# State space layer on one Trainium2 core: the product with C issued one group later, last states copied ahead of the exponentials, six scan buffers

## The chip, the cores and the metric

The kernel runs on one core of one Trainium2 chip. The core has four compute engines that each work through their own list of instructions in order and wait for each other by semaphores: PE (TensorE, matrix products and transposes), DVE (VectorE), ACT (ScalarE) and POOL (GpSimd). Transfers between the chip's main memory and the on-chip memory are issued from a fifth queue, SP. The metric is the device time of one execution in microseconds (us). Before the change it is 8284.29 us, the median of three runs that lay between 8283.61 and 8287.84 us.

## What is computed

The reference is a pair of layers on an image batch of 4 x 384 x 64 x 64 in float32. The second layer, windowed attention, isn't touched by the change. The first is a state space layer: each image is read as 4096 tokens of 384 channels, normalized, projected to 768 inner channels (xb) and 768 gates (z), convolved over four tokens, and passed through a recurrence with 16 states for every inner channel:

```python
xc  = silu(conv(xb) + conv_b)                 # (tokens, 768)
dt, Bm, Cm = split(xc @ x_proj_w.T)           # 24, 16 and 16 columns
dt  = softplus(dt @ dt_w.T + dt_b)            # (tokens, 768)
A   = -exp(A_log)                             # (768, 16)
def step(h, inp):                             # h: (768, 16), one token after another
    dt_t, B_t, C_t, x_t = inp
    dA  = exp(dt_t[:, :, None] * A[None])
    dBx = (dt_t * x_t)[:, :, None] * B_t[:, None, :]
    h   = dA * h + dBx
    y_t = einsum('bdn,bn->bd', h, C_t)
    return h, y_t
y   = (ys + xc * D) * silu(z)
out = y @ out_proj_w.T                        # back to 384 channels, added to the input
```

## The kernel before, as far as the change touches it

The kernel cuts every image into 16 chunks of 256 tokens, 64 chunks in all; the work of one chunk is called a step here. In a step the 768 inner channels are 6 blocks of 128 (one channel for each of the 128 partitions) and the 16 states are 4 groups of 4, so a step has 24 groups, numbered m. A group's scan results lie in a tile `hs` of 128 x (4 states x 256 tokens). Each group takes two slots of the kernel's hand-made schedule, one for each half (two states), so a step has 48 slots. These are the pieces that work on a group:

```python
def dt_x(I, d, h):                 # GpSimd: dt * x of a block
    h["dtx"][d] = ...
    nc.gpsimd.tensor_tensor(h["dtx"][d], dt_block, xc_block, ALU.mult)
def dt_x_copied(d, h):             # ScalarE: a copy in PSUM for VectorE
    nc.scalar.copy(dtx_ps[:, d % 2, :], h["dtx"][d])
def first_states(I, d, h):         # GpSimd: states at the chunk's first token, three small ops
    ...
def begun(I, m, h):                # ScalarE: those into column 0 of db
    nc.scalar.copy(dbs[I, m][:, :, 0], h["h0", d][:, g * NG : (g + 1) * NG])
def driven(I, m, h, eng):          # db = dt*x*B: 16 groups of a step on VectorE, 8 on GpSimd
    db = w2.tile([P, NG, T], F32, tag="db", ..., bufs=6)
    dtx = dtx_ps[:, d % 2, :] if eng is nc.vector else h["dtx"][d]
    eng.tensor_tensor(db[:, :, 1:], dtx..., h["B"][g][:, :, 1:], ALU.mult)
def decay(I, m, half, k, h):       # ScalarE: exp(dt * A) of one state into PSUM
    act(da_ps[half][:, k, 1:], h["dt"][...], AF.Exp, scale=nega[:, d, n : n + 1])
def scans(I, m, half, hs):         # VectorE: the recurrence of two states over 256 tokens
    nc.vector.tensor_tensor_scan(hs[:, pair, :]..., da_ps[half]..., dbs[I, m][:, pair, :]...,
                                 0.0, ALU.mult, ALU.add)
def kept_states(I, m, hs):         # ScalarE: the last token's states, for the next chunk
    nc.scalar.copy(state[:, d, g * NG : (g + 1) * NG], hs[:, :, T - 1])
def with_c(I, m, h, hs):           # GpSimd: hs *= C, in place
    nc.gpsimd.tensor_tensor(hs, hs, h["C"][m % (NS // NG)], ALU.mult)
def summed(I, m, h, hs):           # PE: sum over states, as 8 transposes that accumulate in PSUM
    for k in range(NG):
        for half in range(2):
            nc.tensor.matmul(y[:, d % 2, half, :], hs[:, k, ...], ident, is_transpose=True, ...)
```

Since `with_c` writes over `hs`, it may begin only when `kept_states` has copied the last column. `da_ps` has two tiles, one for each half. After two blocks are summed, `turn` takes the result back to channels: `out` (ScalarE copies the sums, tile `ys`), `back` (PE transposes them and adds xc * D), and `gated` (VectorE multiplies by silu(z), tile `yg`); in the next step the output projection reads `yg`. The loop that puts all of this in order is

```python
            for n in range(STEPS * M):
                I, m = divmod(n, M)
                hs = w2.tile([P, NG, T], F32, tag="hs", name=f"hs_{I}_{m}", bufs=5)
                for half in range(2):
                    others, acts = plan[I][2 * m + half]
                    if half == 0 and behind:
                        acts.insert(0, lambda last=behind[-1]: kept_states(*last[:2], last[3]))
                    if 2 * n + half + 1 < len(halves):
                        nxt = halves[2 * n + half + 1]
                        acts.insert(0, lambda nxt=nxt: decay(*nxt, 0, steps[nxt[0]]))
                        acts.insert(2, lambda nxt=nxt: decay(*nxt, 1, steps[nxt[0]]))
                    for what in acts:
                        what()
                    if half == 0:
                        if behind:
                            with_c(*behind[-1])
                        ready = len(behind) - 1
                        if ready == 1 and behind[0][1] % (2 * NS // NG) == 0:
                            ready = 0
                        for _ in range(ready):
                            summed(*behind.pop(0))
                    scans(I, m, half, hs)
                    for what in others:
                        what()
                behind.append((I, m, steps[I], hs))
```

`acts` is ScalarE's other work of a slot, `others` that of the other engines; both are filled from a table `AT` of slot numbers. So in the first slot of group n ScalarE does one exponential, the copy of group n-1's last states, the other exponential; GpSimd gets the product of group n-1, PE the sums of group n-2, VectorE the scan of group n.

Of the kernel before, what the change touches and what calls it, by code (L numbers as in the profile page):

```python
# [8 lines left out]
F32 = mybir.dt.float32  # L9
# [5 lines left out]
P = 128  # L15
# [7 lines left out]
NG = 4  # L23
# [3 lines left out]
T = 256  # L27
# [21 lines left out]
def two_layers(  # L49
# [45 lines left out]
    def act(o, i, func, **kw):  # L95
        ins = nc.scalar.activation(o, i, func, **kw)  # L96
        return in_order(ins) if func in tabled else ins
# [175 lines left out]
    def layer0(x1s, mvs, gms1):  # L273

        with ExitStack() as es:
# [7 lines left out]
            w2 = es.enter_context(tc.tile_pool(name="w2", bufs=2))  # L283
# [1 line left out]


            AT = {
             'norm': (11, 19, 19, 20, 20, 22, 26, 26, 30, 30, 32),
             'kept': -15,
             'x': ((-11, -11, -8, -7), (-11, -11, -7, -5), (-7, -6, -4, -3)),  # L290
             'c': ((-3, -2, 0, 5), (3, 3, 7, 8), (15, 16, 18, 19)),
             'z': ((1, 2, 3, 5), (10, 11, 14, 15), (8, 15, 16, 18)),
             'burst': (25, 28, 28, 31),
             'softplus': ((31, 33, 34, 36, 36, 37, 39, 39, 42),
                          (44, 47, 47, 50, 50, 51, 52, 52, 55),
                          (57, 60, 61, 61, 63, 65, 66, 66, 69)),
             'dtx': (-5, -3, 9, 13, 23, 29),
             'dtx_ps': (-3, 5, 10, 17, 24, 31),
             'driven': ((-4, 0), (-3, 1), (-1, 1), (-1, 1), (1, 0), (6, 0), (6, 1), (8, 1),
                        (10, 1), (11, 1), (14, 1), (15, 1), (18, 0), (19, 1), (23, 0), (25, 1),  # L300
                        (25, 0), (26, 1), (30, 0), (32, 1), (35, 1), (36, 0), (36, 1),
                        (41, 1)),
             'turn': (21, 24, 26),
             'out': (11, 17, 21, 23, 23, 24, 26, 27, 29, 30),
             'e0': (-4, -2, 11, 12, 23, 26),
             'h0': (-4, -1, 11, 16, 24, 32),
             'first': (-3, 0, 0, 4, 3, 7, 9, 10, 13, 14, 19, 18, 23, 23, 25, 27, 29, 30, 32, 33,
                       38, 41, 41, 46),
            }
            ACT = 1  # L310
# [48 lines left out]
            def bank(tag="mm", pool=ps):  # L359
                return pool.tile([P, 2, T], F32, tag=tag, name=f"{tag}_ps")  # L360
# [282 lines left out]
            def decay(I, m, half, k, h):  # L643

                d, g = divmod(m, NS // NG)
                n = g * NG + 2 * half + k
                act(
                    da_ps[half][:, k, 1:], h["dt"][d // 2][:, d % 2, 1:], AF.Exp,
                    scale=nega[:, d, n : n + 1],
                )  # L650

            def scans(I, m, half, hs):


                pair = slice(2 * half, 2 * half + 2)
                nc.vector.tensor_tensor_scan(  # L656
                    hs[:, pair, :].rearrange("p k t -> p (k t)"),
                    da_ps[half].rearrange("p k t -> p (k t)"),
                    dbs[I, m][:, pair, :].rearrange("p k t -> p (k t)"),
                    0.0, ALU.mult, ALU.add,  # L660
                )

            def kept_states(I, m, hs):
                d, g = divmod(m, NS // NG)
                nc.scalar.copy(state[:, d, g * NG : (g + 1) * NG], hs[:, :, T - 1])  # L665

            def with_c(I, m, h, hs):

                nc.gpsimd.tensor_tensor(hs, hs, h["C"][m % (NS // NG)], ALU.mult)  # L669

            def summed(I, m, h, hs):


                d, g = divmod(m, NS // NG)
                if d % 2 == 0 and g == 0:
                    h["yt"][d // 2] = ps_y.tile([P, 2, 2, P], F32, tag="y", name="y")
                y = h["yt"][d // 2]
                for k in range(NG):
                    first = g == 0 and k == 0
                    last = g == NS // NG - 1 and k == NG - 1  # L680
                    for half in range(2):
                        nc.tensor.matmul(  # L682
                            y[:, d % 2, half, :], hs[:, k, half * P : (half + 1) * P], ident,
                            is_transpose=True, start=(first and half == 0 and d % 2 == 0),
                            stop=(last and half == 1 and d % 2 == 1), skip_group_check=True,
                        )

            def turn(I, p, h, at, s):


                def out():
                    h["ys", p] = w2.tile([P, 2, 2, P], F32, tag="ys", name=f"ys_{I}_{p}")
                    nc.scalar.copy(h["ys", p], h["yt"][p])

                def back():
                    h["y", p] = bank()
                    for k in range(2):
                        y = h["y", p][:, k, :]
                        for half in range(2):
                            nc.tensor.matmul(  # L700
                                y[:, half * P : (half + 1) * P], h["ys", p][:, k, half, :], ident,
                                is_transpose=True, start=(k == 0 and half == 0), stop=False,
                                skip_group_check=True,
                            )
                        nc.tensor.matmul(
                            y, dsd[:, 2 * p + k, :], h["xc"][p][:, k, :], start=False,
                            stop=(k == 1), skip_group_check=True,
                        )

                def gated():  # L710
                    yg = w2.tile([P, 2, T], F32, tag="yg", name=f"yg_{I}_{p}", bufs=4)
                    nc.vector.tensor_tensor(yg, h["y", p], h["sz"][p], ALU.mult)
                    h["yg"].append(yg)

                for after, what, kind in zip(AT["turn"], (out, back, gated), (ACT, 0, 0)):
                    at(s + after, what, kind)
# [63 lines left out]
            for I in range(STEPS):  # L780
                h = steps[I]
# [43 lines left out]
            behind = []  # L825
            for n in range(STEPS * M):
                I, m = divmod(n, M)
                hs = w2.tile([P, NG, T], F32, tag="hs", name=f"hs_{I}_{m}", bufs=5)
                for half in range(2):

                    others, acts = plan[I][2 * m + half]
                    if half == 0 and behind:
                        acts.insert(0, lambda last=behind[-1]: kept_states(*last[:2], last[3]))
                    if 2 * n + half + 1 < len(halves):
                        nxt = halves[2 * n + half + 1]
                        acts.insert(0, lambda nxt=nxt: decay(*nxt, 0, steps[nxt[0]]))
                        acts.insert(2, lambda nxt=nxt: decay(*nxt, 1, steps[nxt[0]]))
                    for what in acts:
                        what()
                    if half == 0:  # L840
                        if behind:
                            with_c(*behind[-1])

                        ready = len(behind) - 1
                        if ready == 1 and behind[0][1] % (2 * NS // NG) == 0:
                            ready = 0
                        for _ in range(ready):
                            summed(*behind.pop(0))
                    scans(I, m, half, hs)
                    for what in others:  # L850
                        what()
                behind.append((I, m, steps[I], hs))
            with_c(*behind[-1])
            for what in behind:
                summed(*what)
            for slot in plan[STEPS]:
# [353 lines left out]
    mvs = [small.tile([P, NJ, 2], F32, tag="mv1", name=f"mv1_{b}", bufs=NB) for b in range(NB)]  # L1210
    gms = [small.tile([P, NJ, 2], F32, tag="gm1", name=f"gm_b{b}", bufs=NB) for b in range(NB)]
    layer0(x1s, mvs, gms)
    only0.close()
    layer1(x1s, mvs, gms)
# [46 lines left out]
```

## Time and profile before

| | before |
|---|---|
| time, median of 3 | 8284.29 us |
| span of the profiled execution | 8282.4 us |
| first layer | until about 5930 us of the span |
| PE busy | 7499.3 us, 91% of the span |
| GpSimd busy | 6954.3 us, 84% |
| VectorE busy | 6666.8 us, 80% |
| ScalarE busy | 6079.0 us, 73% |
| granted TensorE clock, mean | 0.963 |

The shares are averages over two layers with different limits, so the first layer has to be read from its own stretch of the trace. In a view of waits, "DVE hs L656 <- ACT da L96" says that the operation on VectorE which writes `hs` sat idle until ScalarE's operation on `da` ended; then come the total in us, the number of such waits, and the longest. In a timeline, each row is the start, the duration, the engine, the line of the kernel, the operation, what it writes and reads, and in brackets the engine's idle time just before it and what ended it. The lines that matter here are L669 (`with_c`), L665 (`kept_states`), L656 (`scans`), L637 (`driven`), L629 (`begun`), L622 to L625 (`first_states`), L603 and L609 (`dt_x` and its copy), L682 (`summed`), L705 and L712 (`back` and `gated`). L96 is a helper through which ScalarE's functions go, so those are told apart by their tiles.

### The profile page before, as it was taken

How to read it: one execution, taken by the hardware profiler on the slowest of the kernel's cores; microseconds unless marked ns; L12 is line 12 of the kernel's file. 1: busy time of each engine (PE TensorE's matmuls, PEld its weight loads, DVE VectorE, ACT ScalarE, POOL GpSimd, SP SyncE). 2: the span in 40 equal slices, each digit the busy share in tenths (PEclk: the TensorE clock that was granted, in tenths of full speed). 3: DMA queues.
4: the chain of work that ended last, by engine and by line, in shares of the span. 5: the costliest groups of instructions: out<-in, count | busy, mean ns of one | idle time of the engine just before them, and what ended most of it. 6: DMA issues, size and time to landing. Idle time of an engine off the chain costs nothing.

```text
span 8282.4 us, 144249 instructions
## 1 busy us (share of the span) xinstructions
PE 7499.3 (91%) x48570; PEld 5769.9 (70%) x48570; DVE 6666.8 (80%) x9783; ACT 6079.0 (73%) x17509; POOL 6954.3 (84%) x5223
## 2 busy tenths in 40 slices
PE   6898998899998989898989899899799999999999
PEld 5777777777777777777777777777555555555555
DVE  5888888888888888888888888888666666666666
ACT  4888888888888888888888888888555455455455
POOL 3999998989999898999989899999677777677777
PEclk9999999999999999999999999999799999999999
DMA  3212211221222122212211211121222233222322
GB/s 96 77 60 66 77 59 55 66 72 58 65 74 65 55 59 73 64 61 72 68 53 59 66 61 55 60 71 51 79 85 86 85 89 88 81 88 81 87 85 64
DMA packets 459624, 583.93 MB, mean 71 GB/s; under 512 B 195036, under 2 KB 343276, under 8 KB 458756
## 3 DMA queue, kind: packets, MB, share of 16 engines
q1 hardware_dynamic: 458884, 574.69, 22.7%
q8 instruction: 387, 6.34, 0.3%
q14 instruction: 353, 2.89, 0.1%
HBM read 472.02 MB, written 84.73 MB: 67 GB/s over the span
## 4 chain that ended last, share of the span: by engine, by line
PE 44%; ACT 21%; POOL 17%; DVE 12%; issue 5%; DMA 0%; SPq 0%; POOLq 0%; DVEq 0%; ACTq 0%
POOL hs L669 11%; ACT da L96 8%; DVE hs L656 6%; PE mm_ps L419 6%; PE y L682 5%; PE pt_ps L1047 4%; PE mm_ps L574 4%; PE mm_ps L426 3%; PE lg_ps L1016 3%; POOL db L637 3%; PE mm_ps L920 3%; PE mm_ps L1100 3%; PE mm_ps L953 3%; PE mm_ps L983 3%; PE pv_ps L1073 3%
## 5 line engine op out<-in xcount | busy, mean ns | idle before, releaser
L669 POOL TENSOR_TENSOR hs<-hs,C 128x1024 f32<-128x1024 f32 x1536 | 3622.9, 2363 | 478.4 <-ACT state L665 421.2
L656 DVE TENSOR_TENSOR_SCAN hs<-da,db 128x512 f32<-128x512 f32 x3072 | 3623.3, 1211 | 357.8 <-ACT da L96 210.2
L96 ACT ACTIVATE da<-dt,nega 128x255 f32<-128x255 f32 x6144 | 2898.3, 474 | 699.3 <-DVE hs L656 670.8
L1037 POOL TENSOR_SCALAR sg<-sg,rsum 128x308 f32<-128x308 f32 x1536 | 1621.4, 1076 | 638.9 <-DVE rsum L1035 637.2
L682 PE MATMUL y<-ident,hs 128*128 128x128 f32 x12288 | 1667.1, 283 | 468.1 <-POOL hs L669 450.5
L682 PEld LDWEIGHTS y<-ident,hs 128*128 128x128 f32 x12288 | 1443.1, 146 | 728.2 <-POOL hs L669 590.9
L637 DVE TENSOR_TENSOR db<-dtx_ps,B 128x1020 f32<-128x1020 f32 x1024 | 1223.1, 1200 | 110.9 <-ACT dtx_ps L609 105.7
L637 POOL TENSOR_TENSOR db<-dtx,B 128x1020 f32<-128x1020 f32 x512 | 1207.6, 2359 | 1.4 <-DMA B<-bcrows 1.4
L419 PE MATMUL mm_ps<-xn,w_in 128*128 128x256 f32 x4608 | 1160.5, 400 | 1.9 <-DVE xn L390 1.9
L96 ACT ACTIVATE sg<-sg,mx 128x308 f32<-128x308 f32 x1536 | 828.8, 541 | 250.8 <-DVE mx L1022 221.8
L419 PEld LDWEIGHTS mm_ps<-xn,w_in 128*128 128x128 f32 x4608 | 919.6, 206 | 132.3 <-DVE xn L390 2.6
L1022 DVE CUSTOM_DVE_ANT_0 sg<-lg_ps,bias 128x308 f32<-128x308 f32 x1536 | 643.2, 475 | 382.1 <-PE lg_ps L1016 382.1
L426 PE MATMUL mm_ps<-xb,dcv 128*128 128x256 f32 x3072 | 772.7, 400 | 9.4 <-DVE gm_b L270 9.4
L1065 ACT COPY tb<-pt_ps 88x512 f32<-88x512 f32 x384 | 222.3, 579 | 625.5 <-PE pt_ps L1061 625.4
L426 PEld LDWEIGHTS mm_ps<-xb,dcv 128*128 128x128 f32 x3072 | 592.0, 199 | 112.5 <-issue 19.9
L729 PE MATMUL mm_ps<-yg,w_out 128*128 128x256 f32 x2304 | 551.4, 380 | 0.0
L1052 DVE COPY ta<-pt_ps 110x512 f32<-110x512 f32 x768 | 492.7, 683 | 23.3 <-PE pt_ps L1047 23.3
L729 PEld LDWEIGHTS mm_ps<-yg,w_out 128*128 128x128 f32 x2304 | 434.3, 191 | 57.0
L1047 PE MATMUL pt_ps<-ident,sg 128*110 128x128 f32 x3072 | 417.6, 279 | 0.9 <-POOL sg L1037 0.8
L1047 PEld LDWEIGHTS pt_ps<-ident,sg 128*110 128x110 f32 x3072 | 322.8, 133 | 78.0 <-issue 48.4
L920 PE MATMUL mm_ps<-xn,w_qkv 128*128 128x512 f32 (+2 forms) x612 | 277.7, 592 | 60.4 <-DVE xn L907 53.2
L1016 PE MATMUL lg_ps<-k,q 32*128 32x308 f32 x3072 | 311.3, 473 | 0.0
(154 smaller groups left out, 10400.7 us busy)
## 6 DMA issues: line engine op xcount, KB each, us to landing
B<-bcrows SPq DMA_DIRECT2D x256, 512.0 KB
C<-bcrows SPq DMA_DIRECT2D x256, 512.0 KB
vw<-vd SPq DMA_DIRECT2D x1792, 33.0 KB
xr<-x SPq DMA_DIRECT2D x28, 1056.0 KB
vd<-v SPq DMA_DIRECT2D x280, 96.0 KB
xi<-in_x_dram SPq DMA_DIRECT2D x64, 384.0 KB
xo<-in_x_dram SPq DMA_DIRECT2D x64, 384.0 KB
x<-xo SPq DMA_DIRECT2D x64, 384.0 KB
```

What stands on the lines that cost most here:

```text
L96: ins = nc.scalar.activation(o, i, func, **kw)
L419: nc.tensor.matmul(pb[:, k, :], w_in[:, j, m * P : (m + 1) * P], xn[:, j, :], start=(j == 0), stop=(j == NJ - 1),)
L426: nc.tensor.matmul(pb[:, k, :], dcv[:, d, c, :], xb[:, d, c : c + T], start=(c == 0), stop=(c == KC - 1),)
L637: eng.tensor_tensor(db[:, :, 1:], dtx[:, 1:].unsqueeze(1).broadcast_to([P, NG, T - 1]), h["B"][g][:, :, 1:], ALU.mult,)
L656: nc.vector.tensor_tensor_scan(hs[:, pair, :].rearrange("p k t -> p (k t)"), da_ps[half].rearrange("p k t -> p (k t)"), dbs[I, m][:, pair, ...
L669: nc.gpsimd.tensor_tensor(hs, hs, h["C"][m % (NS // NG)], ALU.mult)
L682: nc.tensor.matmul(y[:, d % 2, half, :], hs[:, k, half * P : (half + 1) * P], ident, is_transpose=True, start=(first and half == 0 and d % ...
L729: nc.tensor.matmul(po, w_out[:, d, m * P : (m + 1) * P], h["yg"][d // 2][:, d % 2, :], start=False, stop=(d == ND - 1),)
L1016: nc.tensor.matmul(lg[:, :NK], blk["q"][pr, m, bl, :, :].rearrange("p r c -> p (r c)"), blk["k"][pr, m, :, bl * CB : bl * CB + CW], start= ...
L1022: nc.vector.tensor_tensor_reduce(sg[:, hh, :], lg[:, :NK], bias[:, 4 * m + hh, :], -1.0, BIG, ALU.add, ALU.min, mx[:, hh : hh + 1],)
L1037: nc.gpsimd.tensor_scalar(sg[:, hh, :], sg[:, hh, :], rs[:, hh : hh + 1], None, ALU.mult)
L1047: nc.tensor.transpose(pt[: KN[c], col : col + P], sg[:, 2 * pair + hh, KOFF[c] : KOFF[c] + KN[c]], ident,)
```

## The change

GpSimd's product with C of a group moves one group (two slots) later in GpSimd's list, and PE's sums with it; ScalarE copies a group's last states ahead of both exponentials of the slot instead of between them. The purpose is that GpSimd, when it comes to a product, finds the scan finished and the last states copied. Since results of a scan now stay longer, `hs` gets a sixth buffer of 4 KB for each partition; `ys` goes from two buffers to one and `yg` from four to three (2 KB each) to make room. The table of slots is adjusted: what comes after the sums moves two slots (`turn`), the normalization of a later chunk moves two, and some twenty other entries move by one to three slots. The numbers of groups whose `db` VectorE and GpSimd make stay 16 and 8.

```diff
-             'norm': (11, 19, 19, 20, 20, 22, 26, 26, 30, 30, 32),
+             'norm': (13, 21, 21, 22, 22, 24, 28, 28, 32, 32, 34),
-             'dtx': (-5, -3, 9, 13, 23, 29),
+             'dtx': (-5, -4, 7, 12, 22, 28),
              'dtx_ps': (-3, 5, 10, 17, 24, 31),
-             'turn': (21, 24, 26),
+             'turn': (23, 25, 28),
              'out': (11, 17, 21, 23, 23, 24, 26, 27, 29, 30),
-             'e0': (-4, -2, 11, 12, 23, 26),
-             'h0': (-4, -1, 11, 16, 24, 32),
+             'e0': (-4, -2, 11, 13, 23, 23),
+             'h0': (-4, -1, 11, 16, 24, 35),
 (... and single entries of x, c, z, burst, softplus, driven, first ...)
-    h["ys", p] = w2.tile([P, 2, 2, P], F32, tag="ys", name=f"ys_{I}_{p}")
+    h["ys", p] = w2.tile([P, 2, 2, P], F32, tag="ys", name=f"ys_{I}_{p}", bufs=1)
-    yg = w2.tile([P, 2, T], F32, tag="yg", name=f"yg_{I}_{p}", bufs=4)
+    yg = w2.tile([P, 2, T], F32, tag="yg", name=f"yg_{I}_{p}", bufs=3)
-                hs = w2.tile([P, NG, T], F32, tag="hs", name=f"hs_{I}_{m}", bufs=5)
+                hs = w2.tile([P, NG, T], F32, tag="hs", name=f"hs_{I}_{m}", bufs=6)
-                    if half == 0 and behind:
-                        acts.insert(0, lambda last=behind[-1]: kept_states(*last[:2], last[3]))
                     if 2 * n + half + 1 < len(halves):
                         nxt = halves[2 * n + half + 1]
                         acts.insert(0, lambda nxt=nxt: decay(*nxt, 0, steps[nxt[0]]))
                         acts.insert(2, lambda nxt=nxt: decay(*nxt, 1, steps[nxt[0]]))
+                    if half == 0 and behind:
+                        acts.insert(0, lambda last=behind[-1]: kept_states(*last[:2], last[3]))
                     for what in acts:
                         what()
                     if half == 0:
-                        if behind:
-                            with_c(*behind[-1])
-                        ready = len(behind) - 1
+                        if len(behind) > 1:
+                            with_c(*behind[-2])
+                        ready = len(behind) - 2
 (... unchanged ...)
-            with_c(*behind[-1])
+            for what in behind[-2:]:
+                with_c(*what)
```

## The prediction

> **What bounds the kernel now.** I read the busy shares by slices first, then the busy time of each engine in stretches of the first layer, then the waits of each engine from 1000 to 5000 us, then the timeline around one wait. The slices show two regimes, with a seam in slice 29, near 5930 us; everything below concerns the first. Three stretches of about one step each, with the columns us, then busy us and instruction count of PE, PE's weight loads, DVE, ACT and POOL, then clock and DMA share and GB/s:
>
> ```profile
> 1000.00:1090.00 90.00, 81.38 (x450) 68.55 (x450) 79.59 (x77) 76.42 (x217) 82.20 (x57) 0.96 0.21 67
> 2985.00:3075.00 90.00, 80.97 (x454) 68.23 (x454) 79.42 (x76) 76.84 (x217) 82.22 (x50) 0.98 0.20 61
> 3075.00:3166.00 91.00, 81.70 (x453) 69.21 (x452) 82.85 (x81) 77.63 (x220) 83.34 (x55) 0.96 0.22 69
> ```
>
> The reader is to see that no engine is full: of 271 us together POOL is busy 247.76 (91.4%), PE 244.05, DVE 241.86 (89.2%) and ACT 230.89 (85.2%), and DMA is a fifth. Four nearly full engines are kept from being full by waiting for each other. The waits say how:
>
> ```profile
> POOL hs L669 <- ACT state L665: 304.0, 346, 5.2
> POOL hs L669 <- DVE db L637: 29.9, 44, 0.7
> DVE hs L656 <- ACT da L96: 140.6, 215, 1.2
> DVE yg L712 <- PE mm_ps L705: 136.1, 83, 2.6
> DVE db L637 <- ACT dtx_ps L609: 69.0, 85, 1.1
> DVE hs L656 <- ACT db L629: 67.3, 44, 1.7
> DVE hs L656 <- POOL hs L669: 19.3, 47, 0.9
> ACT da L96 <- DVE hs L656: 460.4, 569, 6.0
> ACT dtx_ps L609 <- POOL dtx L603: 56.8, 41, 1.4
> ACT db L629 <- POOL h L625: 31.0, 41, 0.9
> PE y L682 <- POOL hs L669: 285.3, 204, 2.8
> ```
>
> In these 4000 us there are 2106 scans, 48 to a step, so 43.9 steps of 91.2 us. For one step: POOL waits 304.0 / 43.9 = 6.9 us for the last states (91% of its waits); DVE waits 446 / 43.9 = 10.2 us, of which 3.2 for exponentials, 3.1 for PE's turned sums, 1.6 for dt*x, 1.5 for the first states, 0.4 for a free `hs`, 0.3 unnamed. The waits form a ring: scan, last states, product with C, then whatever stands behind that product in POOL's list. One turn of it in the timeline (POOL, ACT, DVE):
>
> ```profile
> 3027.79 2.36 POOL L669 TENSOR_TENSOR hs<-hs,C 128x1024 f32<-128x1024 f32 x1 [1.42 <-ACT state L665]
> 3030.12 0.33 POOL L622 TENSOR_SCALAR h<-b,dtx 128x16 f32<-128x16 f32 x1
> 3030.48 0.20 ACT L629 COPY db<-h 128x4 f32<-128x4 f32 x1 [0.27 <-POOL h L622]
> 3032.14 2.34 DVE L656 TENSOR_TENSOR_SCAN hs<-da,db 128x512 f32<-128x512 f32 x2 [1.08 <-ACT db L629]
> ```
>
> POOL stood still for 1.42 us with the small first-state operation waiting behind the product; ACT then waited for that operation and DVE for ACT. The product itself was urgent to nobody.
>
> [...] the 0.33 us operation begins only at 3030.12, when the product that had waited 1.42 us is over. [...] two products in a row spanned 4.69 us from 3011.61, so 2.35 us each, against a reported 2.36, and I use 2.36. [...] the products took 2334 to 2410 ns and the scans 1157 to 1226 ns over these 4000 us. So I don't expect denser overlap to lengthen either.
>
> **The change, part by part.** The work is the same: 24 products of 2.36 us, 8 `db` of 2.36 us on POOL and 16 of 1.20 us on DVE, 48 scans of 1.21 us, 24 copies of states in each step. Only waits can change.
>
> 1. *The product one group later.* POOL reaches the product of n-2 in the slot where it used to reach that of n-1. The scan of n-2 and its state copy ended about one group, 91.2 / 24 = 3.8 us, earlier. The mean POOL wait for a state is 304.0 / 346 = 0.88 us, the largest in the timeline of the two steps read here is 2.5 us, and the longest of all is 5.2. So nearly all 6.9 us go as waits in front of products. POOL can't get shorter than its work, 247.76 / 271 x 91.2 = 83.4 us, so this alone allows at most 91.2 - 83.4 = 7.8 us a step, 500 us in 64 steps. It is a ceiling and not the estimate: DVE, which makes the scans, has to keep up.
>
> 2. *What stood behind the product.* `dt_x` and the first states come up to one product and its wait earlier relative to the scans. The DVE waits for `dtx_ps` and for `begun`, 1.6 + 1.5 = 3.1 us a step, are of this kind; the table also moves `dt_x` of four blocks one slot and of one block two slots earlier. I count four fifths as removed: **-2.5 us**.
>
> 3. *PE.* The sums are issued a group later too, so POOL and PE keep their distance of one group; but POOL is no longer held, so PE's 285.3 / 43.9 = 6.5 us of waits for products shrink, and PE is less late where it makes `back`. `gated` now stands three slots behind `back` (25 to 28) instead of two (24 to 26), another 1.9 us. Of DVE's 3.1 us for `yg` I count half: **-1.5 us**. The rest I leave, since PE has 24 input-projection products in a row there, 5.9 us of work that doesn't move.
>
> 4. *States ahead of both exponentials.* The copy takes its place of 0.12 us (its share in the chain of waits) before the first exponential instead of behind it. Both exponentials and the copy wait for the same scan, so a slot's second exponential ends when it did; the order of the two matters to the scan not at all, as it needs both. I count **0**.
>
> 5. *What is given back.* DVE nearer to full means that ACT, busy 85.2% and with only two `da` tiles to work ahead in, is found late more often. If a step goes to 87 us ACT is busy 89%. Today's 3.2 us of waits for `da` I let grow by a third, **+1.1 us**.
>
> 6. *Buffers.* A scan of n needed the sums of n-5, issued in group n-3; now it needs those of n-6, again issued in group n-3. That is neutral, and 0.4 us stay. `ys` is filled at slot 23 and read at 25, and the next comes 16 slots later, so one buffer is enough. `yg`'s first tile of a step is written at slot 28 and the last reader of the three old ones is issued at 26: two slots, 3.8 us, so three are just enough. C's tiles are freed and needed two slots later alike. The end of the layer has one more product to drain, about 4 us once.
>
> Sum: -2.5 - 1.5 + 1.1 = -2.9 us a step; 64 x 2.9 = 186 us, less 4 for the drain, so 182. 8284 - 182 = 8102, said as **8105 us** (-2.2%), with the step at about 88.3 us.
>
> **The rivals.** *POOL as the only bound:* if the ring was what held all four, the step falls towards POOL's 83.4 us; half of the way is 3.9 us, 250 us, and gives 8035; three quarters give 7910. For it: the state wait is 91% of POOL's idle time. Against it: DVE has 10.2 us of waits of its own, of which a third is for exponentials. *The wait only moves:* ACT waits 460.4 / 43.9 = 10.5 us a step for scans, and DVE for ACT, so the scan and the exponentials form an own ring which the change doesn't loosen. If it sets the pace, POOL's wait for states turns into a wait elsewhere (a POOL that runs ahead meets `dt` or `B` that isn't there, since `dt_x` of block 2 moves to slot 7, the very slot where its `dt` is copied), and the time stays at 8240 to 8290. *New waits from the table and the fewer buffers:* `gated` behind the output projection through `yg`, the normalization two slots nearer to the projection that reads it (32 to 34, reader at 37), PE's sums piling up after `turn`. One such stall of 3 us in each step would eat everything: 8300 or a little over. The old table was adapted to the old order; the new one is adapted too, which speaks against this.
>
> **Range and chances.** The middle case is 2.9 us a step. The fast end, 7985, is 4.7 us a step, 60% of the ceiling; the slow end, 8250, is half a microsecond a step, the case where the scan and exponential ring holds. A change of 2% is 166 us or 2.6 us a step, just under my middle: 0.53 for faster by more, 0.38 for within, and 0.09 for slower, which takes a new stall of over 2.6 us in every step after all gains.
>
> **What would show it.** Right: in the changed kernel's waits over 1000 to 5000 us, POOL's wait for states under 60 us; DVE's waits for `dtx_ps` and `db` L629 together under 50 where they were 136; `yg` near 70; POOL's busy share near 94%, its work in a step unchanged; the second layer as long as before. Step 5 is right if `hs` from `da` grows to some 190 us. Wrong: if POOL's idle time stays near 8 us a step under another name, the ring was elsewhere; if products or scans get longer, the overlap costs after all; if `yg` or `hs` waits grow, the buffers do.

## The result, and the profile after

The changed kernel takes **8005.87 us** (median of 4 runs, 8003.15 to 8008.91) against 8284.22 us before: a ratio of **0.9663**, 95% interval 0.9646 to 0.9680, or 278 us less. The prediction was 8105 us with a range from 7985 to 8250. All of the gain lies in the first layer: in the last 2303 us of the span PE is busy 2196.84 us before and 2196.90 us after, VectorE 1478.10 and 1477.91, GpSimd 1639.49 and 1637.14. Three stretches of the same place and length as those shown of before (us; busy us and instruction count of PE, its weight loads, DVE, ACT, POOL; clock, DMA share, GB/s):

```profile
1000.00:1090.00 90.00, 84.33 (x474) 69.02 (x472) 84.76 (x82) 78.52 (x226) 86.84 (x61) 1.00 0.21 67
2985.00:3075.00 90.00, 83.35 (x484) 69.22 (x482) 84.50 (x84) 78.00 (x224) 84.47 (x58) 1.00 0.22 67
3075.00:3166.00 91.00, 85.35 (x483) 70.36 (x484) 85.43 (x83) 80.70 (x234) 87.96 (x63) 1.00 0.23 76
```

All engines are fuller than before, and the granted TensorE clock, 0.96 to 0.98 in those stretches before, is 1.00. In 1000 to 5000 us there are now 2213 scans, 46.1 steps of 86.8 us where there were 43.9 of 91.2: 4.4 us a step less, times 64 is 282. The waits in the same 4000 us (total us, times, longest):

```profile
POOL hs L669 <- ACT state L665: 102.4, 102, 4.8
POOL dtx L603 <- ACT dt L580: 61.7, 49, 2.7
DVE hs L656 <- ACT da L96: 177.0, 336, 1.5
DVE hs L656 <- issue: 31.0, 82, 0.7
DVE hs L656 <- ACT state L665: 29.1, 47, 1.0
DVE hs L656 <- ACT db L629: 7.7, 46, 0.3
DVE db L637 <- ACT dtx_ps L609: 4.5, 3, 1.9
DVE hs L656 <- POOL hs L669: 3.7, 10, 0.4
ACT state L665 <- DVE hs L656: 245.5, 289, 1.9
ACT da L96 <- DVE hs L656: 128.0, 230, 5.6
ACT xc L96 <- PE mm_ps L426: 86.9, 46, 3.0
PE y L682 <- POOL hs L669: 116.6, 167, 1.4
```

GpSimd's wait for the last states fell from 304.0 to 102.4 us. VectorE waits 253.2 / 46.1 = 5.5 us a step instead of 10.2. Its waits for dt*x and for the first states are almost gone (136.3 to 12.2 us together), and the 136.1 us for PE at `yg` are gone altogether. Seven tenths of what is left (177.0 of 253.2 us) is for ScalarE's exponentials. ScalarE has one wait that its list didn't have before, 86.9 us for PE's convolution (`xc`). No wait of PE for a product is longer than 1.4 us; before, the longest was 2.8.

### The profile page after: what moved, and what is told of

The parts are those of the page before. It is cut to its first block, busy times and chain, and to the rows that moved or that the text cites. A ratio compares the mean times of both kernels' runs of the same rounds, so it can differ in the third digit from the quotient of the medians.

```text
span 8003.4 us, 143738 instructions
## 1 busy us (share of the span) xinstructions
PE 7417.0 (93%) x48570; PEld 5588.0 (70%) x48570; DVE 6677.8 (83%) x9783; ACT 6025.3 (75%) x17509; POOL 6933.0 (87%) x5223
## 5 line engine op out<-in xcount | busy, mean ns | idle before, releaser
L656 DVE TENSOR_TENSOR_SCAN hs<-da,db 128x512 f32<-128x512 f32 x3072 | 3663.7, 1213 | 367.8 <-ACT da L96 247.3
L96 ACT ACTIVATE da<-dt,nega 128x255 f32<-128x255 f32 x6144 | 2864.5, 472 | 193.9 <-DVE hs L656 180.3
L682 PE MATMUL y<-ident,hs 128*128 128x128 f32 x12288 | 1607.1, 277 | 227.9 <-POOL hs L669 186.9
L682 PEld LDWEIGHTS y<-ident,hs 128*128 128x128 f32 x12288 | 1385.8, 142 | 510.3 <-POOL hs L669 331.7
L419 PE MATMUL mm_ps<-xn,w_in 128*128 128x256 f32 x4608 | 1100.8, 384 | 58.7 <-ACT sz L96 37.6
L419 PEld LDWEIGHTS mm_ps<-xn,w_in 128*128 128x128 f32 x4608 | 840.0, 191 | 214.3 <-ACT sz L96 62.9
L426 PE MATMUL mm_ps<-xb,dcv 128*128 128x256 f32 x3072 | 722.3, 381 | 0.0
L426 PEld LDWEIGHTS mm_ps<-xb,dcv 128*128 128x128 f32 x3072 | 566.4, 189 | 93.0 <-issue 20.9
L665 ACT COPY state<-hs 128x4 f32<-128x4 f32 x1535 | 299.0, 195 | 360.6 <-DVE hs L656 340.2
L603 POOL TENSOR_TENSOR dtx<-dt,xc 128x256 f32<-128x256 f32 x384 | 280.6, 731 | 109.4 <-ACT dt L580 109.4
```

The costliest lines, as they stand in the source:

```text
L419: nc.tensor.matmul(pb[:, k, :], w_in[:, j, m * P : (m + 1) * P], xn[:, j, :], start=(j == 0), stop=(j == NJ - 1),)
L426: nc.tensor.matmul(pb[:, k, :], dcv[:, d, c, :], xb[:, d, c : c + T], start=(c == 0), stop=(c == KC - 1),)
L656: nc.vector.tensor_tensor_scan(hs[:, pair, :].rearrange("p k t -> p (k t)"), da_ps[half].rearrange("p k t -> p (k t)"), dbs[I, m][:, pair, ...
L682: nc.tensor.matmul(y[:, d % 2, half, :], hs[:, k, half * P : (half + 1) * P], ident, is_transpose=True, start=(first and half == 0 and d % ...
```

## The experiments

Twelve kernels. Each of them is compared with the kernel before on the same chip (8284.7 to 8284.9 us). Runs of one kernel lay up to 13 us apart. "State wait" is GpSimd's wait for the last states and "half clock" the time for which the trace's clock records show TensorE at half speed, both in us within 1000 to 5000 us.

| kernel | us | ratio to before, 95% interval | state wait | half clock |
|---|---|---|---|---|
| before | 8284 | | 304.0 | 324 |
| after | 8005.87 | 0.9663 (0.9646 to 0.9680) | 102.4 | 27 |
| e1_lag: later product only | 8143.41 | 0.9832 (0.9817 to 0.9846) | 121.6 | 195 |
| e2_table: new table only | 8398.18 | 1.0138 (1.0123 to 1.0153) | 370.0 | 341 |
| e3_between: after, ScalarE's order of before | 8043.11 | 0.9706 (0.9690 to 0.9722) | 128.5 | 75 |
| e4_first: ScalarE's new order only | 8163.51 | 0.9854 (0.9839 to 0.9869) | 206.9 | 280 |
| e5_copy_only: only the copy moved | 8226.10 | 0.9929 (0.9914 to 0.9944) | 258.0 | 270 |
| e8_lag_first: after with the old table | 8244.33 | 0.9952 (0.9937 to 0.9967) | 84.5 | 310 |
| e9_after_exps_together: after, exponentials adjacent | 8081.77 | 0.9754 (0.9740 to 0.9769) | 123.2 | 31 |
| e7_five: after, five scan buffers | 8017.66 | 0.9675 (0.9659 to 0.9691) | 104.7 | 34 |
| e10_turn: e8 with the new row turn | 8206.42 | 0.9906 (0.9892 to 0.9921) | 129.2 | 351 |
| e11_old_turn: after, old row turn | 8113.78 | 0.9794 (0.9780 to 0.9809) | 150.6 | 38 |
| e6_warm: before, PE's pauses filled | 8188.56 | 0.9885 (0.9869 to 0.9902) | 240.9 | 41 |
| e12_block0_later: after, one dt*x later | 8004.31 | 0.9662 (0.9648 to 0.9676) | 132.6 | 27 |

My theory was the ring: the product with C stood too early in GpSimd's list and held up what was behind it. The rival was the table: the new slot numbers make the gain. The first four runs take the change apart.

**e1_lag.**

```diff
 (in outline: the kernel after, with the table AT of the kernel before, and)
-                    if half == 0 and behind:        # after the two inserts of decay
-                        acts.insert(0, ... kept_states ...)
+                    if half == 0 and behind:        # ahead of them, as before
+                        acts.insert(0, ... kept_states ...)
```

> The kernel after with the table of slots of the kernel before and the last states copied between the exponentials; only the later product, the later sums and the buffers are left of the change. If the ring through GpSimd is what the change opens, most of the 278 us stay: 8040 to 8110 us, GpSimd's wait for states under 120 us in 4000. If the new table of slots makes the gain, it goes back to 8250 to 8300 us.

Measured: 8143.41 us, 141 less than before. The state wait falls to 121.6 us, so the ring is real and the later product opens it; but this is half the gain, less than the ring theory allowed.

**e2_table.** The kernel before with the whole `AT` of the kernel after, nothing else.

> The kernel before with the new table of slots alone. If the ring is the cause, the table brings little without the later product: 8230 to 8330 us, GpSimd's wait for states stays near 300 us in 4000, and turning the sums back two slots later takes part of the waits for yg. If the table is the cause: 8010 to 8100 us.

Measured: 8398.18 us, 114 *more*. The table alone is worse than I allowed for, which rules out the plain form of the rival. The table is made for another order.

**e3_between.** The kernel after, with the copy inserted ahead of the two `decay` inserts, as before.

> The kernel after with the last states again copied between the two exponentials. Step 4 of the prediction says that the order doesn't matter, as product and scan are served alike: 8006 us, within 8. A rival: the copy in front lets GpSimd run further ahead, and without it 15 to 40 us are lost.

Measured: 8043.11 us, 37 more than after. The claim that ScalarE's order doesn't matter falls.

**e4_first.** The kernel before, with the copy inserted behind the two `decay` inserts, as after.

> The kernel before with the last states copied ahead of both exponentials, nothing else. There the product waits for the copy, which now comes 0.37 us earlier. If the ring is the cause, each of some 346 waits in 4000 us gets shorter by up to 0.37 us, 2.9 us a step of GpSimd's idle time, of which a third to a half reaches the end: 8190 to 8235 us. If GpSimd's wait for states was harmless: 8284 us, within 8.

Measured: 8163.51 us, 121 less: more than my upper figure, for one small copy per group. The state wait, at 206.9 us, explains only a part. The edit does more than move the copy. The second `decay` is put in at place 2 of the list. With the copy in the list already, place 2 is right behind it; without it, ScalarE's first other operation of the slot comes ahead. So the order of the first slot of each group was exponential, copy, exponential, other; it is now copy, exponential, *other*, exponential. Two things had moved, and e5 and e9 part them.

**e5_copy_only.**

```diff
 (the kernel e4_first, and)
-    acts.insert(2, lambda nxt=nxt: decay(*nxt, 1, steps[nxt[0]]))
+    acts.insert(2 if half else 1, lambda nxt=nxt: decay(*nxt, 1, steps[nxt[0]]))
```

> The kernel before with the last states copied ahead of both exponentials, and the two exponentials of a group's first slot kept next to each other. In the change, and in the run with the copy ahead alone (8163.5 us), ScalarE's first other operation of that slot also came to stand between the two exponentials. If the earlier copy itself makes that gain, since GpSimd's product may begin some 0.4 us earlier, this kernel keeps most of it: 8140 to 8190 us. If it came from the other operation being served earlier (states of the first token, dt*x, inputs of the convolution), it falls back to 8250 to 8290 us.

Measured: 8226.10 us, between the two expectations. The copy's place gives 58 us of the 121, the other operation between the exponentials the remaining 63.

**e9_after_exps_together.** The same one-line edit in the kernel after.

> The kernel after with the two exponentials of a group's first slot next to each other, the copy still ahead of both. If only the copy's place matters: 8000 to 8012 us, or a few us less since the second scan gets its exponential earlier. If the other operation between them matters: 8025 to 8050 us, near the 8043 us of the run with the copy between the exponentials.

Measured: 8081.77 us, 76 more than after, and 39 more than e3, which has the copy between. So in the kernel after, moving the copy alone from between the exponentials to the front of them (e3 to e9) loses 39 us, and moving the other operation between them (e9 to after) gains 76: the worth of ScalarE's new order lies in what stands between the exponentials. The timeline of ScalarE in e9 (start us, duration, operation, pieces merged) shows one possible reason:

```profile
3005.41 0.20 ACT L665 COPY state<-hs 128x4 f32<-128x4 f32 x1 [0.24 <-DVE hs L656]
3005.51 0.98 ACT L96 ACTIVATE da<-dt,nega 128x255 f32<-128x255 f32 x2
```

The same work in the kernel after:

```profile
3004.98 0.20 ACT L665 COPY state<-hs 128x4 f32<-128x4 f32 x1 [1.60 <-DVE hs L656]
3005.08 0.47 ACT L96 ACTIVATE da<-dt,nega 128x255 f32<-128x255 f32 x1
3005.49 0.35 ACT L609 COPY dtx_ps<-dtx 128x256 f32<-128x256 f32 x1
3005.78 0.87 ACT L96 ACTIVATE da<-dt,nega 128x255 f32<-128x255 f32 x2
```

In e9 two exponentials of one slot in a row take 0.98 us; the second, 0.48 us long, starts 0.98 - 0.48 = 0.50 us after the first. In the kernel after an exponential is followed 0.41 us later by another operation, and the pair in the last line, which writes into two different `da` tiles, takes 0.87 us. Twenty-four pairs at 0.1 us are 2.4 us a step; ScalarE's busy time is 3532.29 / 45.5 = 77.6 us a step in e9 and 76.0 in the kernel after. Its 1.6 us and the lost 1.2 us a step (76 / 64) are of one size. That the shared tile is the cause of the longer pair wasn't tried, and the way from there to the scans isn't shown: VectorE's waits for exponentials are shorter in e9 (148.0 us) than in the kernel after (177.0).

**e8_lag_first.** The kernel after with the whole old table.

> The kernel after with the old table of slots. The later product alone took 141 us off and ScalarE's new order alone 121 us. If they open different waits, the sum stands: 8010 to 8035 us, and the new table adds almost nothing. If both act on the same wait of GpSimd for the last states, together they give little over the larger one: 8090 to 8140 us, and the table is worth some 100 us to the later product although it costs 114 us without it.

Measured: 8244.33 us, only 40 less than before and *worse than either part alone*. Neither expectation foresaw that. Its waits say where it went, though GpSimd's wait for states is the lowest of all, 84.5 us:

```profile
DVE yg L712 <- PE mm_ps L705: 137.7, 88, 4.2
PE mm_ps L574 <- DVE spe L564: 182.7, 83, 2.6
ACT ys L693 <- PE y L682: 49.8, 55, 4.7
POOL dtx L603 <- ACT dt L580: 145.7, 84, 4.2
```

The ring is open, the wait for `yg` is as long as before (136.1), and three other waits have come in the ring's place. The sums come later, but ScalarE's copy of them (`ys`) stands at its old slot and stops ScalarE; what stands behind it may be late for that reason, `dt` first, and so GpSimd's dt*x. But e1 has the same later sums with the same old table (its waits for `ys` are 31.3 us, those for `dt` 66.2) and is 101 us faster. Why ScalarE's new order costs 101 us there, where it gains 121 in the kernel before and 37 with the new table, isn't shown.

**e10_turn** and **e11_old_turn** take one row of the table each way. In the new row ScalarE's copy and VectorE's gating stand two slots later, PE's turning back (`back`) only one.

```diff
 (e10_turn: the kernel e8_lag_first, and)
-             'turn': (21, 24, 26),
+             'turn': (23, 25, 28),
 (e11_old_turn: the kernel after, and the reverse)
```

> The later product and ScalarE's new order with the old table of slots, except that the row turn is the new one (23, 25, 28 instead of 21, 24, 26). With the old row the two together took only 40 us off (8244 us), and ScalarE stood waiting for the sums at the copy to ys. If the row turn, which has to follow the later sums, is what the table was needed for: 8030 to 8090 us. If the gain lies in the other entries: 8200 to 8250 us.

> The kernel after with the row turn of the kernel before (21, 24, 26). If this row is what the later sums need, most of its share is lost: 8100 to 8200 us, with waits for yg near 130 us in 4000 again. If not, 8005 to 8030 us.

Measured: 8206.42 and 8113.78 us. The row is worth 38 us with the old table and 108 us with the new one. In e10 the waits for `yg` are almost gone, and others stand in their place:

```profile
DVE hs L656 <- ACT da L96: 265.3, 311, 3.9
DVE db L637 <- ACT dtx_ps L609: 109.5, 42, 2.8
DVE yg L712 <- PE mm_ps L705: 6.5, 9, 0.9
ACT xb L96 <- PE mm_ps L419: 153.4, 45, 4.3
```

ScalarE now stands 3.5 us a step for PE's input projection (17.6 us in 4000 before). So `turn` has to follow the sums, but the other entries are worth another 200 us (8206.42 to 8005.87). Which of them isn't settled; I didn't try them singly. In e11 I had expected waits for `yg` near 130 us. They were 9.5 us; instead ScalarE waited 49.1 us for the sums at `ys`, and VectorE 87.6 us for nothing that the profile names (31.0 in the kernel after) and 35.6 us for first states (7.7).

**e7_five.** The kernel after with `bufs=5` for `hs`.

> The kernel after with five scan buffers instead of six. A scan then waits for sums that are issued two groups before it instead of three. By step 6 the sixth buffer only keeps the distance, so VectorE's waits for a free hs grow from under 0.1 us a step to 1 to 3 us: 8060 to 8200 us. If GpSimd and PE are so much on time that one group less of room is enough: 8006 us, within 8.

Measured: 8017.66 us (8009.98 to 8018.71), 12 more than after. VectorE's wait for GpSimd's use of `hs` is 5.3 us against 3.7, so the room is hardly used. The sixth buffer is worth about 12 us of the 278, no more than the distance between runs of one kernel.

**e6_warm** asks why the waits for `yg` vanished altogether. In the kernel before, PE's timeline has pauses that end with slow transposes, and behind them comes the block of 24 products of the input projection (L419):

```profile
3006.92 1.09 PE L682 MATMUL y<-ident,hs 128*128 128x128 f32 x8
3010.79 1.97 PE L682 MATMUL y<-ident,hs 128*128 128x128 f32 x8 [2.78 <-POOL hs L669]
3012.55 6.10 PE L419 MATMUL mm_ps<-xn,w_in 128*128 128x256 f32 x24
```

After a pause of 2.78 us the same eight transposes took 1.97 us instead of 1.09.

```diff
 (the kernel before, with a tile zeros, and in summed)
+                for _ in range({5: 10, 15: 16}.get(m, 0)):
+                    nc.tensor.matmul(
+                        y[:, d % 2, 0, :], zeros, ident, is_transpose=True, start=False,
+                        stop=False, skip_group_check=True,
+                    )
                 for k in range(NG):
```

> The kernel before with transposes of a tile of zeros added into y ahead of the sums of groups 5 and 15 of each step, 10 and 16 of them, where PE stood idle 1.9 and 2.8 us and its next 8 transposes took up to 1.97 instead of 1.09 us. The result is the same sum. If the lower granted clock after such pauses is what makes PE late for yg, the mean clock in the first layer goes from 0.96 to over 0.98, the waits for yg fall from 136 to under 80 us in 4000, and the time to 8190 to 8250 us. If the clock is only an effect of the waits: 8280 to 8340 us, with the added transposes at most in the way.

Measured: 8188.56 us, 96 less than before, with 26 useless transposes *added* to every step; PE's work grows and the kernel is faster. The place in the trace of e6, where lines are numbered a little higher, and the block of 24 in the next step:

```profile
3010.25 1.25 PE L681 MATMUL y<-ident,zeros 128*128 128x128 f32 x10
3012.35 1.09 PE L689 MATMUL y<-ident,hs 128*128 128x128 f32 x8 [0.85 <-POOL hs L671]
3052.86 5.34 PE L421 MATMUL mm_ps<-xn,w_in 128*128 128x256 f32 x24
```

The pause that is left is 0.85 us, and the transposes behind it take 1.09 us. Over 4000 us the half clock falls from 324 to 41 us, the block of 24 takes 5.34 us in each of two steps of e6 where it took 6.68 us on average, and the waits for `yg` fall from 136.1 to 62.5 us, while GpSimd's wait for states, 240.9 us, is still four fifths of what it was. So the clock is a cause of its own.

It isn't the only one at `yg`. In e8, which has the old row `turn`, a block takes 5.35 us, as in e6 within 0.01, and still VectorE waits 137.7 us there; in e10 the new row takes this to 6.5. The block in e8, and the wait for `yg` in e6:

```profile
2990.08 5.35 PE L419 MATMUL mm_ps<-xn,w_in 128*128 128x256 f32 x24
DVE yg L719 <- PE mm_ps L712: 62.5, 47, 1.7
```

**e12_block0_later.** In the kernel after GpSimd stands for `dt` at the first block's dt*x (61.7 us).

```diff
-             'dtx': (-5, -4, 7, 12, 22, 28),
+             'dtx': (-4, -4, 7, 12, 22, 28),
```

> The kernel after with dt*x of a step's first block one slot later (-4 instead of -5), behind a product instead of ahead of it. In the kernel after GpSimd stands there 1.2 to 2.8 us for dt, 61.7 us in 4000. If GpSimd, busy 95%, is what bounds the step, most of this comes back: 7950 to 7990 us. If the scans and their exponentials set the pace, the time stays at 8000 to 8010 us; if VectorE then waits for this dt*x, 8010 to 8040 us.

Measured: 8004.31 us, the same as after. GpSimd's waits in e12:

```profile
POOL hs L669 <- ACT state L665: 132.6, 150, 4.8
POOL e L624 <- ACT e L96: 21.1, 44, 0.5
POOL dtx L603 <- ACT dt L580: 4.4, 6, 1.0
```

Of the 57 us taken from the last line, 50 turn up in the two others (102.4 and 1.3 us in the kernel after). GpSimd, busy 95.3% in the kernel after, isn't what bounds the step; it arrives early and waits elsewhere. That the scans and their exponentials set the pace fits this, but no run tests it alone.

## Why the prediction came out as it did

The direction and the mechanism of steps 1 and 2 were right, step 4 was wrong, and the size was too small: 2.9 us a step were predicted and 4.4 measured. Point by point:

- **Step 1, the ring.** Right. The state wait falls from 6.9 to 102.4 / 46.1 = 2.2 us a step, and with the later product alone to 121.6 us in 4000. I had said "nearly all" and under 60 us; a third stayed. GpSimd seems to run ahead until it meets a state that isn't copied yet: in e12, where it stands less at dt*x, this wait grows to 132.6 us. As a ceiling the step held: 4.4 us gained of 7.8 allowed.
- **Step 2, what stood behind the product, -2.5 us.** Right in kind and size: 136.3 / 43.9 = 3.1 us a step became 12.2 / 46.1 = 0.3, so -2.8.
- **Step 3, PE, -1.5 us.** This term was mis-sized. All of the 3.1 us went, not half. I left half to the input projection behind the pause as 5.9 us of work that doesn't move; but that block took 6.68 us on average before, 5.49 on average in the kernel after and 5.34 in two steps of e6. Before, its first products ran at the half clock (in the place shown 0.43 us apart until 3014.07 us and 0.22 from then on). In e6, which fills the pauses, the waits for `yg` fall to 62.5 / 44.6 = 1.4 us a step, so by my estimate the clock is worth about 3.1 - 1.4 = 1.7 of the 3.1. What took the other 1.4 isn't settled: with the old table it is the row `turn` (137.7 to 6.5 us from e8 to e10), but with the new table hardly any of these waits come back without that row (9.5 us in e11). The granted clock before was known (0.963 on average), and the term has nothing in it for PE's rate after a wait.
- **Step 4, ScalarE's order, 0.** This failed. I wrote that "the order of the two matters to the scan not at all", and looked at the two exponentials and the copy only. The edit also put another operation between the exponentials. Undoing the whole order costs 37 us in the kernel after (e3), and undoing only that operation's place 76 (e9); in the kernel before, the whole order gains 121 us (e4) and the copy alone 58 (e5).
- **Step 5, given back, +1.1 us.** Right in kind: waits for `da` went from 3.2 to 3.8 us a step, those without a name from 0.3 to 0.7, and those for the copy of states, new on the list, are 0.6. Together 3.5 to 5.1, so +1.6 us.
- **Step 6, buffers, 0.** Right: no wait for a free `ys`, `yg` or `hs` of size appeared, and the sixth buffer is worth 12 us.

With the measured sizes the sum is -2.8 - 3.1 + 1.6 = -4.3, and another -0.4 for waits on `hs` from GpSimd: -4.7, against 4.4 from the spacing of the steps. Of the remaining 0.3, 0.2 is idle time that the list of waits doesn't hold (0.1 us a step before, 0.3 after), the rest rounding and 0.06 us more work. That a denser overlap would lengthen neither products nor scans was my estimate from how long they took before; from 1000 to 5000 us they took 2333 to 2415 and 1162 to 1226 ns in the kernel after. One small reading was off as well: the two products from 3011.61 span 4.69 us, so their starts are 4.69 - 2.36 = 2.33 us apart and not 2.35, which changes no term.

Of the rivals, the POOL bound is ruled out for the kernel after by e12. "The wait only moves" is right in what it named (GpSimd does meet `dt` that isn't there, at the first block and not at block 2 as I wrote, and scan and exponentials now hold each other) and wrong in the size. "New waits from the table" describes e2, where VectorE waited 96.1 us at the normalization that the table had moved, but not the change as a whole. I had looked at the table as an adjustment of small entries. It is worth 238 us to the two code changes (8244.33 to 8005.87), and costs 114 without them. The parts of this change don't add up: -141 for the later product, -121 for ScalarE's order, -40 for both with the old table, -278 with the new one.

## What to carry to other kernels

When engines that are each 85 to 91% busy wait for each other in turn, look for the operation that waits though nobody is in need of its result, and issue it later; then move what follows it as well, because the parts of such a change can be worth less than nothing one by one. Look at the rate of PE's work just behind its waits: here a pause of 2.78 us cost a second time, as the eight transposes behind it took 1.97 us instead of 1.09, and filling two pauses of each step with harmless work was a cheap test (96 us less in e6). And read an edit to an ordered list by what the list finally holds, not by the item that was moved.

## What the runs showed of the hardware

- In the kernel before, from 1000 to 5000 us, eight transposes of 128x128 took 1.47 to 1.97 us after each of 41 waits of 2.48 to 2.78 us for the product with C, 1.97 us after three of 2.01 us, and 1.09 us after 82 of 0.70 to 1.32 us. Of 41 waits of 1.92 to 1.94 us, two were followed by slow ones (1.73 and 1.75 us). After two waits of 2.25 and 2.26 us for the copy to `ys` the first eight took 1.06 us, so the length of the last wait alone didn't decide.
- The clock records before and after have two values only, full and half; the half ones lasted 3.41 us or multiples of it, but for one at the end of each span (3.59 and 2.20 us). They fit the slow work: one stands from 3010.66 to 3014.07 us, the slow transposes begin at 3010.79, and the starts of the products behind them are 0.43 us apart until 3014.07 and 0.22 us from then on. The records of this trace begin at whole multiples of 3.41 us from each other, and whether the place of a pause between these marks matters wasn't tried.
- Two exponentials of 128x255 that stood next to each other started 0.49 to 0.52 us apart where both wrote into one PSUM tile (187 of 188 pairs from 1000 to 5000 us of the kernel after) and 0.40 to 0.42 us apart in most pairs that wrote into two (415 of 510); an exponential was followed by another operation after 0.41 us (the median of 3394).
